# Attention product of a transformer block on one core: token blocks in twos with seven products, the second layernorm's statistics for two chunks at once, and the last weight look-ups moved beside the first part of the down projection

## The chip, the core and the metric

The kernel runs on one core of a Trainium2 chip. The core has engines with queues of their own, which work at the same time and wait for each other through semaphores: TensorE (PE in the profile; PEld are its weight loads), VectorE (DVE), ScalarE (ACT), GpSimd (POOL) and SyncE (SP). Each queue runs its instructions in the order in which they were written. DMA transfers are issued from the SP, ACT and POOL queues. TensorE writes to PSUM, which is read and written by DVE and ACT as well; the rest of the work lies in SBUF, and larger intermediate results go through DRAM.

The metric is the time of one execution on the device in microseconds, the median of several runs. The profile is one further execution, with its own time.

## The reference

All tensors are fp32, `x` is (2, 2048, 512). What is computed, cut to what matters:

```python
def attention(x, Wq, Wk, Wv, Wo):          # x: layernorm of the input
    q, k, v = x @ Wq, x @ Wk, x @ Wv
    qT, kT, vT = swapaxes(q), swapaxes(k), swapaxes(v)
    scores = einsum('bes,bfs->bef', qT, kT) / sqrt(16)
    out = einsum('bef,bfs->bes', softmax(scores), vT)
    return swapaxes(out) @ Wo

def ffn(x, lut, gate_idx, up_idx, down_idx):    # a weight is lut[idx], 16 values
    h = silu(x @ lut[gate_idx].T) * (x @ lut[up_idx].T)      # 1376 features
    return h @ lut[down_idx].T

x = x + attention(layernorm(x), Wq, Wk, Wv, Wo)
x = x + ffn(layernorm(x), lut, gate_idx, up_idx, down_idx)
```

The scores are taken between features (512 x 512 per batch), not between tokens. So attention can be folded into one 512 x 512 matrix for each batch.

## The kernel before

**Tiling.** The 4096 tokens of the two batches are 8 chunks (`NCH`) of 512 tokens, each of 4 blocks (`J`) of 128 tokens; 32 blocks (`NBLK`) in all, four chunks to a batch. `x` stays in SBUF throughout. A "512-column" operand is 128 partitions by 512 fp32.

**Stages, in order on PE.**
1. The first layernorm (class `Norm`, L185), and from its result n the Gram matrix n^T n of each batch.
2. Four 512 x 512 products per batch (class `Square`, `square()`), each by seven products of half size in place of eight (Strassen's scheme in Winograd's form), with the softmax in between. The last ones give m, one matrix per batch (`m_sb`).
3. The y stage: for each block, y = n m is added to x. `y_product` (L834) issues four matmuls of 128 x 512, with a transposed block of n as the weights; `n_turned` makes that block by a DVE transpose (`turn`, L823) of what `n_load` read back from DRAM (`nd`). 32 blocks make 128 matmuls. `added` (L843) adds y to x on DVE (L846), which also leaves the row sum `total`. From that the second layernorm's statistics are made on ACT, in `Norm.sums`: the mean (`mul`, L211), and a Square with an accumulated sum (L212). After each fourth block there is one square root (L216), then `rest` (a few small DVE operations, L231 to L248); `f_normed` writes the normed block (L278, ACT) and stores pairs of blocks to DRAM (`xnd`, L267), `f_load` reads a chunk back on the POOL queue, and `f_turned` transposes it on DVE, which gives the operand `xb` of the next stage. `f_sums` makes sums and differences of two chunks for that stage's scheme of seven products.
4. The gate/up stage: 10 slices of 128 features (`f`) by four pairs of chunks (`p`). A unit `GateUp(f, p)` is again seven products, each of several matmuls of 128 x 512, run by `Line.run` in the order a1, c1, a4 of the unit before, a2, c2, b, a3. `units` (L1413) lists them; the first eight go (0,0), (1,0), (0,1), (0,2), (0,3), (1,1), (1,2), (1,3).
5. The `rows` stage (L1349): the last 96 features.
6. The down projection, part 0 and part 1, each for eight chunks (`Down`).

**Look-ups.** The weights of stages 4 to 6 are made from indices on DVE. A `Job` (L285) reads two blocks of indices (`fetch`, L299, a DMA on the POOL queue into a single buffer), makes a 16-bit copy on ACT (`cast`, L303), and then runs 19 steps on DVE: four preparing operations (L315 to L322), eight `leaf` operations (L330) and seven `copy_predicated` picks (L342). The generator `looked_up` yields these steps one at a time; at its sixteenth step a job issues the fetch of the next one. `jobs` (L416) sets the order: gate/up pairs 0 and 1, down 0, down 2, gate/up pair 2, down 4, the other gate/up pairs, and then down 6, 8 and 10. The down jobs' weights are stored to DRAM (`wdd`) and loaded again before the down stage.

**What sets the order.** All engines' instruction order is written out at build time. In stages 2 and 3 `pump(x)` takes look-up steps worth x units of DVE time: in the y stage 1.6 for each of the first 16 blocks and 1.0 for the other 16. `side(k)` (L902) lists what else goes beside block k. In stages 4 to 6 a planner with a clock for PE and one for DVE (`clock`) decides: `between` takes one waiting operation (`todo`), and then `fill(lead)` issues look-up steps as long as the DVE clock is not further than `lead` ahead of the PE clock. `late` (L1387) puts what remains of the y stage's work (`side(32)` to `side(39)`, transposes, sums) into `todo`. Loops of the form `while …: step()` issue look-up steps at once, whatever the planner's clock says: before the down stage, all that remain.

Of the kernel before, what the change touches and what calls it, by code (L numbers as in the profile page):

```python
# [69 lines left out]
def tile_attn_ffn(  # L70
# [47 lines left out]
    wdd = dram.tile([P, NFT, E], F32, tag="wdd", name="wdd")  # L118
# [66 lines left out]
    class Norm:  # L185
        def __init__(self, c, name, back=None):
            self.name, self.back = f"{name}{c}", back
            if back:
                self.std, self.mean = back.rstd, back.nmr
            self.rstd = const.tile([P, J], F32, tag=f"rstd_{self.name}", name=f"rstd_{self.name}")  # L190
            self.nmr = const.tile([P, J], F32, tag=f"nmr_{self.name}", name=f"nmr_{self.name}")
            self.minus, self.scale = -1.0, 1.0
# [10 lines left out]
        def sums(self, j, total, block):  # L203

            if j == 0:
                self.mv = small.tile([P, J, 2], F32, tag="mv", name=f"mv_{self.name}")
                self.r0 = small.tile([P, J], F32, tag="r0", name=f"r0_{self.name}")
                self.q = small.tile([P, J], F32, tag="q", name=f"q_{self.name}")
            mean, var = self.mv[:, j, 0:1], self.mv[:, j, 1:2]
            junk = xnp.tile([P, E], BF16, tag="junk", name=f"junk_{self.name}_{j}", bufs=1)  # L210
            nc.scalar.mul(mean, total, -1.0 / E)  # L211
            nc.scalar.activation(junk, block, AF.Square, bias=mean, accum_out=var)  # L212
            self.minus, self.scale = 1.0, 1.0 / E

        def sqrt(self, a, b):
            nc.scalar.activation(self.r0[:, a:b], self.mv[:, a:b, 1], AF.Sqrt, bias=eps_sb, scale=self.scale)  # L216
# [15 lines left out]
        def rest(self, a, b, between=lambda: None):  # L232
# [5 lines left out]

            if self.scale != 1.0:
                nc.vector.tensor_scalar_mul(var, var, self.scale)  # L240
# [4 lines left out]
            stt(nmr, mean, self.minus, rstd, ALU.mult, ALU.mult)  # L245
            if self.back:
                nc.vector.reciprocal(self.std[:, a:b], rstd)
                nc.vector.tensor_scalar_mul(self.mean[:, a:b], mean, -self.minus)  # L248

        def pair(self, j, block, quarters=False):  # L250


            if j % 2 == 0:
                self.xn = xnp.tile([P, KB, 2, P], F32, tag="xn", name=f"xn_{self.name}_{j}", bufs=2)
            to = self.xn[:, :, j % 2, :]
            if quarters:
                to = to.rearrange("p i (m a) -> p m i a", a=Q)
                block = block.rearrange("p (m i a) -> p m i a", i=KB, a=Q)
            else:
                block = block.rearrange("p (i e) -> p i e", i=KB)  # L260
            self.normed(j, block, to)
            return self.xn
# [6 lines left out]
        def undone(self, j, xn, to):  # L269
# [4 lines left out]
                bias=self.mean[:, j : j + 1], scale=self.std[:, j : j + 1],  # L274
            )

        def normed(self, j, block, to):
            nc.scalar.activation(  # L278
                to, block, AF.Identity, bias=self.nmr[:, j : j + 1],
                scale=self.rstd[:, j : j + 1],  # L280
            )
# [104 lines left out]
    def down_job(i):  # L386

        f0, rows = FT[i]
# [3 lines left out]
        def dest():  # L392
            if i < K1:
# [6 lines left out]
        def after():  # L400
            nc.sync.dma_start(wdd[:rows, i : i + k, :], made[0])
# [3 lines left out]
        turn = NFT + (i - K1) // 2  # L405
        return Job(f"wd{i}", rows, E, loads, dest, after, lambda: i < K1 or turn < 4 + ended[0])
# [9 lines left out]
    jobs = [pair_job(0), pair_job(1), down_job(0), down_job(2)]  # L416
    for f in range(2, NFT - 1):
        jobs.append(pair_job(f))
        if f == 2:
            jobs.append(down_job(4))  # L420
    jobs += [pair_job(NFT - 1), *(down_job(i) for i in range(K1, NFT, 2))]
# [87 lines left out]
    ln2 = [Norm(c, "f", back=ln1[c]) for c in range(NCH)]  # L509
# [19 lines left out]
    class Operand(dict):  # L529
# [3 lines left out]
        def new(self, tag):  # L533
            self[tag] = sums.tile([P, 2, H], F32, tag="e", name=f"{tag}_{self.name}")
            return self[tag]
# [17 lines left out]
    def right(t, name, order=("T2", "T4", "T1")):  # L553
# [3 lines left out]
        def t3():  # L557
            for tag in order:
                o.new(tag)
# [157 lines left out]
    def square(a, b, dest, name, beside, rate=(0.7,) * 7):  # L717
# [5 lines left out]
        stages = [u.a1, u.c1, last.a4 if last else lambda: None, u.a2, u.b1, u.c2, u.a3]  # L723
        for i, stage in enumerate(stages):
# [3 lines left out]
            pump(rate[i])  # L728
# [77 lines left out]
    nls, nTs, ys, xfs, fls = {}, {}, {}, {}, {}  # L806
    xb, xs = {}, {}
# [17 lines left out]
    N_AT = ("a0", "a1", "a0", "a1", "a2", "a3", "a1", "a3")  # L825

    def n_load(c):
        nls[c] = reload(room(N_AT[c], f"nl_{c}"), nd[c], nc.sync)

    def n_turned(k):  # L830
        if k < NBLK:
            nTs[k] = sums.tile([P, KB, P], F32, tag="e", name=f"nT_{k}")
            turn(nTs[k], nls[k // J][:, k % J])

    def y_product(k):
        ys[k] = bank(f"y_{k}")
        m = m_sb[k // (J * CPB)]
        for i in range(KB):
            nc.tensor.matmul(  # L839
# [926 lines left out]
```

## Time and profile before

| | |
|---|---|
| median of 3 runs | 1063.83 us (1063.69 to 1063.89) |
| profiled execution | 1064.37 us, its span 1062.6 us |
| granted TensorE clock | 1.00 |
| y stage on PE | 174.7 to 286.3 us, with the last product of the squares and 256 records of y |
| gate/up stage | 286.3 to 747.6 us |
| `rows` stage | 747.6 to 789.0 us |
| down stage | 789.0 to 1058.5 us |

A span runs from the first to the last recorded instruction of the profiled execution; what lies around it belongs to the execution's time. In the tables of stages each row has a stretch of time and its length, and then the busy time of PE, of its weight loads, and of DVE, ACT and POOL, each with the number of instructions in brackets, the granted clock, the DMA share and the rate. In a row of the groups, the text has the line of the source, the engine, the operation, the output and the inputs with their shape, and the count; after the first bar the busy time and the mean duration of one instruction in ns, after the second the idle time before them on their engine and what ended it. In a timeline each row has a start, a duration, the engine and line; "x18" stands for 18 instructions of the kind run back to back. An fp32 matmul has two records on PE.

### The profile page before, as it was taken

What the parts mean: (1) busy time and instruction counts of PE and PEld (TensorE: products, weight loads), DVE (VectorE), ACT (ScalarE), POOL (GpSimd) and SP (SyncE); (2) the same over time, 40 slices, a digit from 0 to 9 for tenths busy, and PEclk for the clock granted to TensorE, in tenths of its full rate; (3) what the DMA queues carried; (4) which work ended last, traced back from release to release, by engine and by line L of the source; (5) the groups of instructions that cost most, each with busy time, mean ns of one, the idle gap of its engine ahead of it and who ended that gap; (6) DMA issues with size and microseconds to landing.
All of it is one profiled execution on the core that took longest, in us unless ns stands there. A gap on an engine that the chain in (4) does not pass through costs nothing.

```text
span 1062.6 us, 11343 instructions
## 1 busy us (share of the span) xinstructions
PE 1055.5 (99%) x3554; PEld 661.3 (62%) x3554; DVE 803.3 (76%) x1538; ACT 385.1 (36%) x725; POOL 108.6 (10%) x160
## 2 busy tenths in 40 slices
PE   8999999999999999999999999999999999999998
PEld 5668887444444444444444444444998888888887
DVE  7888788898998897887988868849756455656554
ACT  4652532455542224444443444444222222211111
POOL 0000000012120120230141023014000000000000
PEclk9999999999999999999999999999999999999999
DMA  8650314589571366696697679569747665666773
GB/s 342 224 186 21 74 25 119 137 225 250 153 217 41 133 232 197 166 201 209 198 188 215 199 170 222 190 205 195 238 149 244 204 211 187 194 195 203 226 227 117
DMA packets 129084, 194.69 MB, mean 183 GB/s; under 512 B 18992, under 2 KB 59184, under 8 KB 127872
## 3 DMA queue, kind: packets, MB, share of 16 engines
q1 hardware_dynamic: 75904, 105.81, 31.4%
q0 software_dynamic: 15776, 39.92, 17.9%
q10 hardware_dynamic: 37344, 48.24, 14.0%
q8 instruction: 28, 0.46, 0.2%
q14 instruction: 32, 0.26, 0.1%
HBM read 111.42 MB, written 82.51 MB: 183 GB/s over the span
## 4 chain that ended last, share of the span: by engine, by line
PE 97%; DVE 1%; ACT 1%; DMA 0%; issue 0%; SPq 0%; ACTq 0%
PE a_g L1065 22%; PE a_d L1065 14%; PE y L839 10%; PE c_g L1065 8%; PE c_d L1065 7%; PE gp L522 6%; PE rows L1349 4%; PE b_d L1065 4%; PE x_g L1065 4%; PE z_g L1065 4%; PE w_g L1065 3%; PE b_g L1065 2%; PE ea_t L675 1%; PE ea_p L675 1%; PE ea_m L675 1%; PE ea_s L675 1%
## 5 line engine op out<-in xcount | busy, mean ns | idle before, releaser
L839 PE MATMUL y<-m,nT 128*128 128x512 f32 x256 | 110.2, 592 | 0.0
L342 DVE COPY_PREDICATED w<-b_w,w 128x1024 f32<-128x1024 int16 (+1 forms) x77 | 98.6, 1280 | 1.4
L839 PEld LDWEIGHTS y<-m,nT 128*128 128x128 f32 x256 | 48.5, 190 | 60.5 <-issue 57.3
L1065 PE MATMUL a_g<-xT_a,s 128*128 128x512 f32 x160 | 75.5, 594 | 0.0
L1065 PE MATMUL a_g<-xb,w 128*128 128x512 f32 x160 | 75.3, 593 | 0.0
L1065 PE MATMUL c_g<-xb,w 128*128 128x512 f32 x160 | 75.2, 592 | 0.0
L1065 PE MATMUL a_d<-dT,hs_a 128*128 128x256 f32 x288 | 72.6, 379 | 0.0
L522 PE MATMUL gp<-xn_a 128*128 128x128 f32 (+3 forms) x256 | 69.9, 434 | 1.7 <-DVE xn_a L223 1.7
L330 DVE TENSOR_SCALAR w<-idx_w,lut_x,lut_sb 128x1024 int32<-128x1024 int32 (+1 forms) x88 | 67.7, 794 | 0.2
L522 PEld LDWEIGHTS gp<-xn_a 128*128 128x128 f32 x256 | 43.9, 190 | 28.4 <-issue 15.1
L172 DVE TENSOR_TENSOR r<-r,p_d 128x256 f32<-128x256 f32 x64 | 27.1, 424 | 44.4 <-ACT p_d L181 41.5
L1065 PEld LDWEIGHTS a_d<-dT,hs_a 128*128 128x128 f32 x288 | 54.5, 189 | 7.7
L1065 PE MATMUL a_g<-xT_sq,s 128*128 128x512 f32 x120 | 56.7, 595 | 0.0
L181 ACT COPY p_d<-a_d 128x256 f32<-128x256 f32 x32 | 11.9, 372 | 121.4 <-PE a_d L1065 121.4
L1065 PEld LDWEIGHTS a_g<-xT_a,s 128*128 128x128 f32 x160 | 30.1, 190 | 38.9 <-issue 36.4
L1065 PEld LDWEIGHTS a_g<-xb,w 128*128 128x128 f32 x160 | 30.3, 190 | 38.5 <-issue 35.9
L1065 PEld LDWEIGHTS c_g<-xb,w 128*128 128x128 f32 x160 | 30.4, 190 | 38.3 <-issue 37.3
L342 DVE COPY_PREDICATED wd<-b_wd,wd 128x1024 f32<-128x1024 int16 (+1 forms) x42 | 50.7, 1208 | 0.8
L172 DVE TENSOR_TENSOR r<-r,a_d 128x256 f32<-128x256 f32 x64 | 26.8, 419 | 29.5 <-PE a_d L1065 29.5
L181 ACT COPY u<-a_g 128x512 f32<-128x512 f32 x40 | 23.4, 586 | 59.9 <-PE a_g L1065 57.3
L172 DVE TENSOR_TENSOR c<-a_g,p 128x512 f32<-128x512 f32 x40 | 27.6, 691 | 20.4 <-PE a_g L1065 19.0
L1349 PEld LDWEIGHTS rows<-last,xb 128*128 128x128 f32 x256 | 41.7, 190 | 0.5 <-issue 0.5
(357 smaller groups left out, 2086.2 us busy)
## 6 DMA issues: line engine op xcount, KB each, us to landing
hd<-h SPq DMA_DIRECT2D x80, 256.0 KB, 3.3
h<-hd SPq DMA_DIRECT2D x40, 512.0 KB, 6.3
nl<-nd SPq DMA_DIRECT2D x32, 256.0 KB, 5.8
xnd<-xn_f ACTq DMA_DIRECT2D x16, 512.0 KB, 4.6
fl<-xnd POOLq DMA_DIRECT2D x32, 256.0 KB, 6.1
xn_back<-xnd SPq DMA_DIRECT2D x32, 256.0 KB, 4.0
rd<-r SPq DMA_DIRECT2D x32, 256.0 KB, 3.2
r<-rd SPq DMA_DIRECT2D x32, 256.0 KB, 4.5
```

The costliest lines, as they stand in the source:

```text
L172: nc.vector.tensor_tensor(dest, a, b, op)
L181: nc.scalar.copy(dest, a)
L330: vec.tensor_scalar(dest.bitcast(I32), idx, lut_x[:rows, k : k + 1], lut_i[:rows, at : at + 1], ALU.bitwise_and, ALU.bitwise_xor,)
L342: vec.copy_predicated(dest, masks[level - 1], t)
L522: nc.tensor.matmul(gp[b][i][:, i * P :], xn[:, i, j % 2, :], xn[:, i:, j % 2, :], start=c % CPB == 0 and j == 0, stop=c % CPB == CPB - 1 a ...
L675: nc.tensor.matmul(ps[:, m, :], self.a[a][:, k, m * P : (m + 1) * P], self.b[b][:, k, :], start=first and m == k == 0, stop=k == 1, skip_g ...
L839: nc.tensor.matmul(ys[k], nTs[k][:, i, :], m[:, i, :], start=(i == 0), stop=(i == KB - 1))
L1065: nc.tensor.matmul(ps, lhsT, rhs, start=first and i == 0, stop=i == len(pairs) - 1, skip_group_check=not first,)
L1349: nc.tensor.matmul(ps[:, jj, :], x[:, j * P : (j + 1) * P], w, start=i == 0, stop=i == len(pairs) - 1,)
```

## The change

**The y stage.** Two blocks j and j+2 of a chunk form a pair (class `Pair`). Their two rows of n times the four quarters of m are made by seven products in place of eight, with the same scheme as the squares. Each product is two matmuls of 128 x 256: 16 pairs by 14 make 224 matmuls. A pair has one PSUM tile of three banks, from a pool `yps` with two buffers. ACT copies the running sum `a` within the tile to `c11` (after a1), to `c21` (after a2) and to `c22` (after a3); DVE adds the seventh product, `p7`, to both halves of block j+2 (`seventh`); `added(1)` and `added(0)` then add the blocks j+2 and j to x and issue their statistics on ACT. Class `Chunk` transposes a chunk's blocks and makes four sums of n for it on DVE; `m_ops` has four sums of each m, those of m_0 in the last square and those of m_1 in steps 1 to 4.

**The second layernorm.** Class `Rows` has the statistics of two chunks (eight columns) in place of one chunk's four: four square roots and four `rest` in place of eight. The values that undo the norm (reciprocal and negative mean) are made at the end of the `rows` stage (`turn_back`).

**Look-ups.** `pump` is no longer called in the y stage, and the last square's rates are mostly 0. `jobs` becomes gate/up pairs 0 to 3, down 0, the remaining pairs, down 2 to 10; down 6, 8 and 10 come in the first part of the down stage, and write into `wd2` in SBUF, with no way through DRAM. There `lead` is 1.2, and 0.7 after it. Look-up steps are issued at once after unit (0,3) until down 0 is done (ahead of the release of `xnp`), before the `rows` stage until down 4 is done, and at the beginning of the down stage's second part.

**Units.** The first eight go (0,0), (1,0), (0,1), (1,1), (0,2), (0,3), (1,2), (1,3), and `late` has other contents: what remains of the norms, transposes 8 to 31, and the sums of pairs 1 to 3. `SUMS_AT`, `f_place` and the places of `n_load` use other buffers.

The diff, cut to its core:

```diff
-    wdd = dram.tile([P, NFT, E], F32, tag="wdd", name="wdd")
+    wdd = dram.tile([P, K1, E], F32, tag="wdd", name="wdd")
...
+        def sums(self, k, total, block):
+            mean = self.mean[:, k : k + 1]
+            junk = xnp.tile([P, E], BF16, tag="junk", name=f"junk_{self.name}_{k}", bufs=1)
+            nc.scalar.mul(mean, total, -1.0 / E)
+            nc.scalar.activation(
+                junk, block, AF.Square, bias=mean, accum_out=self.var[:, k : k + 1]
+            )
+
+        def sqrt(self):
+            nc.scalar.activation(self.r0, self.var, AF.Sqrt, bias=eps_sb, scale=1.0 / E)
+
+        def rest(self):
+            r0, q, stt = self.r0, self.q, nc.vector.scalar_tensor_tensor
+            nc.vector.reciprocal(r0, r0)
+            stt(q, self.var, EPS * E, r0, ALU.add, ALU.mult)
+            stt(q, q, -0.5 / E, r0, ALU.mult, ALU.mult)
+            stt(self.rstd, q, 1.5, r0, ALU.add, ALU.mult)
+            nc.vector.tensor_tensor(self.nmr, self.mean, self.rstd, ALU.mult)
+
...
+        def turn_back(self):
+            nc.vector.reciprocal(self.rstd, self.rstd)
+            nc.vector.tensor_scalar_mul(self.mean, self.mean, -1.0)
+
...
-            if i < K1:
+            if i >= K1:
+                t = wd2[0][:, i - K1 : i - K1 + k, :]
+            elif i == 0:
                 t = xnp.tile([P, 2, E], F32, tag="wds", name=f"wd_{i}", bufs=1)
             else:
...
+            if i < K1:
+                nc.sync.dma_start(wdd[:rows, i : i + k, :], made[0])
+            done.append(i)
             yield 0.1
 
         loads = [down_idx[f0 + P * q : f0 + P * q + rows, :] for q in range(k)]
-        turn = NFT + (i - K1) // 2
-        return Job(f"wd{i}", rows, E, loads, dest, after, lambda: i < K1 or turn < 4 + ended[0])
+        turn = NFT + (i - 2) // 2
+        gate = (lambda: turn < 4 + ended[0]) if 0 < i < K1 else (lambda: i == 0 or bool(wd2))
+        return Job(f"wd{i}", rows, E, loads, dest, after, gate)
+
...
-    jobs = [pair_job(0), pair_job(1), down_job(0), down_job(2)]
-    for f in range(2, NFT - 1):
-        jobs.append(pair_job(f))
-        if f == 2:
-            jobs.append(down_job(4))
-    jobs += [pair_job(NFT - 1), *(down_job(i) for i in range(K1, NFT, 2))]
+    jobs = [pair_job(f) for f in range(4)] + [down_job(0)]
+    jobs += [pair_job(f) for f in range(4, NFT)] + [down_job(i) for i in range(2, NFT, 2)]
...
-    N_AT = ("a0", "a1", "a0", "a1", "a2", "a3", "a1", "a3")
-
-    def n_load(c):
-        nls[c] = reload(room(N_AT[c], f"nl_{c}"), nd[c], nc.sync)
-
-    def n_turned(k):
-        if k < NBLK:
-            nTs[k] = sums.tile([P, KB, P], F32, tag="e", name=f"nT_{k}")
-            turn(nTs[k], nls[k // J][:, k % J])
-
-    def y_product(k):
-        ys[k] = bank(f"y_{k}")
-        m = m_sb[k // (J * CPB)]
-        for i in range(KB):
-            nc.tensor.matmul(
-                ys[k], nTs[k][:, i, :], m[:, i, :], start=(i == 0), stop=(i == KB - 1)
...
+            def s3():
+                one, two = parts
+                self.of.update({
+                    "11": one[:, 0:2], "12": one[:, 2:4], "S3": two[:, 0:2], "22": two[:, 2:4],
+                })
+                sub(two[:, 0:2], one[:, 0:2], two[:, 0:2])
+
+            of = self.of
+            return [lambda j=j: turned(j) for j in range(J)] + [
+                s3, lambda: sub(made("S2"), of["22"], of["S3"]),
+                lambda: add(made("S1"), of["S2"], of["11"]),
+                lambda: sub(made("S4"), of["12"], of["S2"]),
+            ]
+
...
+    class Pair:
+
+
+
+
+        def __init__(self, n):
+            self.c, self.s = divmod(n, 2)
+            self.k = J * self.c + self.s
+            self.n, self.m = chunks[self.c].of, m_ops[self.c // CPB]
+            t = self.t = yps.tile([P, 3, E], F32, tag="y", name=f"y_{n}", bufs=2)
+            self.c11, self.a, self.p7 = t[:, 0, H:], t[:, 1, :H], t[:, 1, H:]
+            self.c21, self.c22 = t[:, 2, :H], t[:, 2, H:]
+
+        def mm(self, to, a, b, first=False):
+            for k in range(2):
+                nc.tensor.matmul(
+                    to, self.n[a][:, k, self.s, :], self.m[b][:, k, :],
+                    start=first and k == 0, stop=k == 1, skip_group_check=not first,
+                )
+
+        def a1(self):
+            self.mm(self.a, "11", "11", True)
+            nc.scalar.copy(self.c11, self.a)
+
+        def c1(self):
+            self.mm(self.p7, "S3", "T3")
+
+        def a2(self):
+            self.mm(self.a, "S2", "T2")
+            nc.scalar.copy(self.c21, self.a)
+
+        def b(self):
+            self.mm(self.c11, "12", "21")
+
+        def a3(self):
+            self.mm(self.a, "S1", "T1")
+            nc.scalar.copy(self.c22, self.a)
+
+        def c2(self):
+            self.mm(self.c21, "22", "T4")
+
+        def a4(self):
+            self.mm(self.a, "S4", "22")
+
+        def seventh(self):
+            to = block(self.k + 2).rearrange("p (e h) -> p e h", e=2)
+            add(to, to, self.p7.unsqueeze(1).to_broadcast([P, 2, H]))
+
+        def added(self, i):
+            k, of = self.k + 2 * i, self.t[:, 2, :]
+            if not i:
+                of = self.t[:, 0:2, :].rearrange("p b e -> p (b e)")[:, H : H + E]
+            total = small.tile([P, 1], F32, tag="total", name=f"total_{k}")
+            nc.vector.scalar_tensor_tensor(
+                block(k), of, 1.0, block(k), ALU.mult, ALU.add, accum_out=total
             )
-
...
-    for k in range(NBLK):
-        if k:
-            n_turned(k + 1)
-        y_product(k)
-        if k == 0:
-            before[0].a4()
-            n_turned(1)
-            n_load(1)
+        0: turns_of(0, 2), 1: turns_of(0, 2), 2: [lambda: n_load(1), *turns_of(0, 2)],
+        3: [*turns_of(0, 1), m_ops[0].todo[0]], 4: [m_ops[0].todo[1]],
+        5: [*turns_of(0, 1), m_ops[0].todo[2]], 6: [m_ops[0].todo[3]],
+    }, (0.7, 0.7, 0, 0, 0, 0, 0), final=True)
+    pps.release()
+    yps = tc.alloc_tile_pool(name="yps", bufs=1, space=PSUM, reuse_waits="tile")
+
+    def norms(n):
+
+        i, at = divmod(n - 4, 4)
+        ops = []
+        if at == 0 and 0 <= i < NPR:
+            ops.append(ln2[i].sqrt)
+        if at == 1 and 0 <= i < NPR:
+            ops.append(ln2[i].rest)
+        i, at = divmod(n - 6, 4)
+        if 0 <= i < NPR:
+            ops += [lambda k=2 * J * i + 2 * at + q: f_normed(k) for q in range(2)]
+        c = (n - 8) // 2
+        if n % 2 == 0 and 0 <= c < NCH:
+            ops.append(lambda: f_load(c))
+        return ops
+
+    turned_at = {10: [0], 11: [1], 12: [2], 13: [3], 14: [4, 5, 6], 15: [7]}
+    summed_at = {15: 2}
+    NST = NBLK // 2
+    y = None
+    for n in range(NST):
+        work = turns_of(n // 2 + 1, 4) if n // 2 + 1 < NCH else []
+        if 1 <= n < 5:
+            work.append(m_ops[1].todo[n - 1])
+        work += [lambda k=k: f_turned(k) for k in turned_at.get(n, ())]
+        work += [lambda: next(f_pairs[0])] * summed_at.get(n, 0)
+        side = norms(n)
+        last, y = y, Pair(n)
+        y.a1()
+        if work:
+            work.pop(0)()
+        if last:
+            last.c2()
+            last.a4()
+            last.added(1)
+        if n % 2 == 0 and n // 2 + 2 < NCH:
+            n_load(n // 2 + 2)
+        y.a2()
+        if last:
+            last.added(0)
+        if work:
+            work.pop(0)()
+        if n == NST - 1:
+            y.c1()
+            y.a3()
+            y.b()
         else:
-            if k % J == 3 and k // J + 2 < NCH:
-                n_load(k // J + 2)
-            side(k)
-        pump(1.6 if k < LAG else 1.0)
...
+    next(f_pairs[0])
+    next(f_pairs[0])
+    for n, k in zip(((16,), (17,), (18,), (19,), (20, 21), (22,), (), ()), range(2 * J, 4 * J)):
+        late(normed=n, turned=[k])
+    for p in range(1, NPR):
+        late(pair=p)
+        late(pair=p)
+        late(pair=p, times=2)
+        if p == 1:
+            late(turned=[16, 17])
+            late(turned=[18, 19])
+            for k in range(20, 24):
+                late(turned=[k])
+        elif p == 2:
+            for k in (24, 26, 27, 28, 30):
+                late(turned=[k, k + 1] if k in (24, 28, 30) else [k])
 
 
...
-    units = [(0, 0), (1, 0), (0, 1), (0, 2), (0, 3), (1, 1), (1, 2), (1, 3)]
+    units = [(0, 0), (1, 0), (0, 1), (1, 1), (0, 2), (0, 3), (1, 2), (1, 3)]
...
-        if (f, p) == (1, 1):
+        if (f, p) == (0, 3):
+            while 0 not in done:
+                step()
...
+    while K1 - 2 not in done:
+        step()
...
-    while step() is not None:
-        pass
-    assert next(lookup, 0) == 0
 
...
-    leads[0] = 0.7
+    leads[0] = 1.2
...
-                nc.sync.dma_start(wd2[0][:, : NFT - K1 - 1, :], wdd[:, K1 : NFT - 1, :])
-                nc.sync.dma_start(wd2[0][:LAST, NFT - K1 - 1, :], wdd[:LAST, NFT - 1, :])
+            if (part, c, jj) == (1, 0, 0):
+                while step() is not None:
+                    pass
+                assert next(lookup, 0) == 0
+                leads[0] = 0.7
             if (part, c, jj) == (0, NCH - 1, 0):
+                while NFT - 3 not in done:
+                    step()
```

## The prediction

> **What bounds the kernel now.** I read the busy totals and the chain of waits first, then the table by stage, then the timeline around y and around the squares.
>
> ```profile
> PE 1055.5 (99%) x3554; PEld 661.3 (62%) x3554; DVE 803.3 (76%) x1538; ACT 385.1 (36%) x725; POOL 108.6 (10%) x160
> ...
> PE 97%; DVE 1%; ACT 1%; DMA 0%; issue 0%; SPq 0%; ACTq 0%
> ```
> ```profile
> 174.70:286.30 111.60, 111.60 (x265) 49.89 (x264) 100.93 (x222) 54.01 (x126) 15.30 (x27) 1.00 0.72 183
> 286.30:747.60 461.30, 461.30 (x1074) 202.99 (x1074) 384.56 (x579) 189.97 (x322) 89.18 (x121) 1.00 0.68 187
> ```
> The chain is PE from end to end, at clock 1.00. In the y stage (first row: length; then PE, PEld, DVE, ACT, POOL) PE has no gap, with DVE busy 101 of 112 us. So PE work saved is time saved, but only while nothing else makes PE wait: any wait adds in full.
>
> One place of the squares shows PE waiting for a copy that stands behind other work in ACT's queue:
>
> ```profile
> 116.96 1.67 PE L675 MATMUL ea_s<-p,S_wq 128*128 128x256 f32 x7
> ...
> 117.35 0.71 ACT L746 ACTIVATE a<-a,nb 128x512 f32<-128x512 f32 x1
> ...
> 118.05 0.56 ACT L687 COPY a<-ea_s 128x512 f32<-128x512 f32 x1
> ...
> 118.67 0.94 PEld L675 LDWEIGHTS ea_s<-T_p,S_wq 128*128 128x128 f32 x5 [0.43 <-ACT a L687]
> ```
> The copy could not start before the exponential ended, and PE began 0.06 us after the copy.
>
> **Prices.** From the y stage, the groups and the DMA list:
>
> ```profile
> 208.65 7.89 PE L839 MATMUL y<-m,nT 128*128 128x512 f32 x18
> ...
> 212.03 0.20 ACT L211 ACTIVATE mv_f<-total 128x1 f32<-128x1 f32 x1
> ...
> 212.26 0.72 ACT L212 ACTIVATE junk_f<-x,mv_f 128x512 bf16<-128x512 f32 x1
> ...
> 212.98 0.80 ACT L278 ACTIVATE xn_f<-x,nmr_f,rstd_f 128x512 f32<-128x512 f32 x1
> ...
> 214.53 0.65 DVE L846 SCALAR_TENSOR_TENSOR x<-y,x 128x512 f32<-128x512 f32 x1
> ...
> 215.12 1.53 DVE L330 TENSOR_SCALAR w<-idx_w,lut_x,lut_sb 128x1024 int32<-128x1024 int32 x2
> 215.23 0.20 ACT L211 ACTIVATE mv_f<-total 128x1 f32<-128x1 f32 x1 [1.45 <-DVE x L846]
> ```
> ```profile
> L839 PE MATMUL y<-m,nT 128*128 128x512 f32 x256 | 110.2, 592 | 0.0
> L342 DVE COPY_PREDICATED w<-b_w,w 128x1024 f32<-128x1024 int16 x70 | 91.4, 1306 | 1.3
> L172 DVE TENSOR_TENSOR c<-a_g,p 128x512 f32<-128x512 f32 x40 | 27.6, 691 | 20.4 <-PE a_g L1065 19.0
> L181 ACT COPY p_d<-a_d 128x256 f32<-128x256 f32 x32 | 11.9, 372 | 121.4 <-PE a_d L1065 121.4
> L303 ACT CAST b_w<-idx_w 128x1024 int16<-128x1024 int32 x10 | 10.4, 1041 | 2.2 <-DMA idx_w<-in_up_idx_dram 0.9 <-ACT xn_f L278 0.6 <-ACT xn_a L278 0.6
> ```
> ```profile
> idx_w<-in_up_idx_dram POOLq DMA_DIRECT2D x9, 256.0 KB, 5.0
> ```
> A matmul has two records. 512 columns: (7.89 − 0.592)/17 = 0.429 us a record, 0.858 a matmul. 256 columns, from the x7 line and the page's 379 ns for one: (1.67 − 0.379)/6 = 0.215, 0.432 a matmul. Hand-overs: a DVE add's start to ACT's mul 0.70 (214.53 to 215.23); mul and Square until ACT's next operation 0.95 (212.03 to 212.98); ACT end to PE 0.05; PE end to DVE or ACT 0.20 to 0.27, ACT end to DVE 0.03 and DVE end to PE 0.06 (starts against ends elsewhere in the same timeline). Leaf to leaf (1.53 − 0.805, one leaf's mean) 0.72, a pick 1.20 (its start to the next one's) to 1.31.
>
> **1. The products.** 128 matmuls of 512 columns become 224 of 256: 128 × 0.858 = 109.9 us become 224 × 0.432 = 96.8. Minus 13.1 us, 6.05 us of PE a step (one step is one pair of blocks, seven products of 0.864).
>
> **2. The hand-overs inside a step.** In the changed kernel's instruction order PE runs a1(n), c2(n−1), a4(n−1), a2(n), c1(n), b(n), a3(n). All of a pair lies in one PSUM tile of three banks, and an instruction waits for the last one of another engine that touched the tile. Two waits close a ring:
> - c2(n−1) waits for `seventh` on DVE, which waits for the copy to c22 on ACT, which waits for a3(n−1): 0.20 + 0.37 + 0.03 + 0.69 + 0.06 = 1.35 us. Only a1(n), 0.86, covers it: PE waits 0.49.
> - c1(n) waits for the copy to c21. On ACT that copy stands behind mul and Square of `added(1)`, which waits for a4(n−1). From a4's end: 0.25 + 0.70 + 0.95 + 0.37 + 0.05 = 2.32 us, covered by a2(n), 0.86: PE waits 1.46. Queued behind c1 are b and a3, and so the next c22 copy: the next step's wait is not shortened.
>
> The copy to c11 is covered by c2 and a4 (1.73), in even steps too, with two `normed` (0.80 each) and the `xnd` issue of some 0.5 in front of it, though only just. The `nl` loads stay 32 on SP, two chunks ahead (5.8 us to land): 0. A step takes 6.05 + 0.49 + 1.46 and some 0.1 for two restarts, whose first weight load is not hidden: 8.1 us. Neither engine is the bound (by these rows DVE has 4.6 to 5.9 us a step, ACT 4.6 to 4.9); the ring is. Between `seventh` and `added(1)` DVE also has three or four operations of 0.6 to 0.7 (the four transposes and four new sums of the next chunk over two steps): in steps 1 to 4 (sums of the second m) and 10 to 12 (a transpose) a fourth one makes `added(1)` late by 0.4, the `rest` in steps 5 and 9 by 0.65 each, step 13's by 1.25: 7 × 0.4 + 1.3 + 1.25 = 5.4 us.
>
> Sum of the stage: 0.85 at the start (the first copy waits for the last work of m_1), step 0, which has no other pair to cover its copies, 4.32 + 1.3 = 5.6; 15 × 8.1 = 121.5; 5.4; 3.1 for the last c2, a4 and adds. Together 136.4, against 109.9: plus 26.5 net, that is 39.6 of waits against 13.1 saved. Lower end: both adds' hand-overs at their smallest readings, no restarts and no late DVE work, 15 × 7.7 and 2 for those extras, 127 (+17). Upper: 0.3 us more a step, 142 (+32).
>
> The Trainium skill (Perfetto Trace Analysis, § Matmuls) says that independent matmul groups should rotate through PSUM banks so that ACT and DVE empty one while the next runs. The 0.43 us wait above is this case's own instance of what else happens. By the rule the pairs' two tiles would hide the copies, and the stage would be PE's 97 us; but four of the seven products of a pair go through one bank here, so the rule speaks against this layout. No number of the sum needs it.
>
> **3. The look-ups forced after unit (0,3).** With no look-ups in y, the loop that completes the first `down` job must issue its 15 remaining steps (8 leaves, 7 picks) at once: 8 × 0.72 + 7 × 1.25, some 14.6 us of DVE, which no unit covers in PE's order. But DVE is not what is late first: the next job's index fetch, on POOL, waits for the last leaf, the twelfth of these steps (8 × 0.72 + 4 × 1.25 = 10.8 us), and DVE first has four adds of 0.69 of unit (0,3): 13.5 us after that unit's a3. Issue 0.54, landing 5.0, the cast 1.04, and behind the cast on ACT a 512-column copy, 0.59, which PE's c2 of unit (1,2) waits for: 20.7. PE runs out of work after four products of 4 × 0.429, 6.86 us. Wait: 14. If the fetch landed early, DVE's backlog would still hold unit (1,2)'s a4 by some 11; late picks, 17.
>
> **4. The rest.** Eight `sqrt`/`rest` sets become four (0.3 and some 1 us each, off PE): 0. Transposes and sums moved from y into the first gate/up units, and the normed blocks of y's end waiting for two xn buffers until `xnd` is stored (4.6 us for 512 KB): DVE there has 385 of 461 us, 0 to 5, I take 2. The look-ups beside `down`'s first part, about 41 us of DVE (three jobs) where that engine is at 151 of 269 us over the stage: 0 to 6, I take 1; where the planner is late, the flush at that part's end pays 1.2 a pick. Their index fetches come behind the gate/up ones on POOL and are no longer followed by stores on SP and a load of `wd2`: hidden behind PE, 0. The row stage loses its look-ups, where PE is full anyway: 0.
>
> Sum: 1062.6 − 13.1 + 39.6 + 14 + 2 + 1 = 1106.1 span. The profiled run was 1064.37 with that span, the median 1063.83, 1.2 above it: **1107**.
>
> **The rivals.**
> - A, the forced look-ups are absorbed (the fetch lands in time and PE has other work): 1107 − 14 = 1093. For it: DVE idles 77 us in gate/up. Against: the queues are strict and the order is fixed. 0.13.
> - B, y costs what PE costs: 96.8 + 4 at its ends, and only the forced steps are paid: 1063.8 − 9 + 14 + 3 = 1072. For it: the copies are 0.37 and ACT is idle half the stage. Against: the order of ACT's queue. 0.04.
> - C, the other side: the copies and adds are hidden in y and the forced steps too: 1063.8 − 13.1 + 4 = 1055. What decides is the step: at 6.7 us the stage is 0.85 + 4.32 + 15 × 6.7 + 1.7 = 107.4 and 2.5 us are left for everything behind it; above that, or with a forced block over 3, the gain is gone. For it: PE alone needs 6.05. Against: point 2. 0.05.
> - D, DVE falls behind in gate/up and in `down`, and PE waits there in many places: +8 to +15, 1115 to 1122. For it: 41 us of look-ups and bunched transposes. Against: from `f` = 2 on, the planner is where it was. 0.06.
>
> **How the numbers follow.** The main case 0.72, at 1107, own range 1096 to 1118; A 0.13, B 0.04, C 0.05, D 0.06. The low end 1089 takes in A and the lower end of y with 11 of forced steps; the high end 1119 holds the upper ends of y and of the forced steps with most of D. Less than 0.2% (2.1 us) can't be told from no change here; B's and C's edges leave 0.02 for it. Faster 0.05, same 0.02, slower 0.93.
>
> **What would show it.** y: 97 us of PE in about 136, with some 1.5 us before c1 put down to ACT and 0.5 before c2 put down to DVE, step by step; if PE's idle there is under 15 us, ring and price are wrong. After unit (0,3): DVE full with L330/L342 for about 15 us and one gap of PE of 11 to 17 us, ended by ACT. Gate/up from `f` = 2 and `rows`: as before. `down`: PE idle under 6 us. A PE gap elsewhere of over 5 us would make the forecast wrong.

## The result, and the profile after

| | before | changed |
|---|---|---|
| median | 1063.86 us (1063.69 to 1063.96, 4 runs) | 1120.68 us (1119.62 to 1122.28, 4 runs) |
| ratio, with 95% interval | | 1.0536 (1.0517 to 1.0554) |
| profiled execution, span | 1064.37, 1062.6 | 1119.62, 1117.6 |
| first gate/up record, from the span's start | 286.3 | 312.9 |
| gate/up stage | 461.2 | 488.5 |
| `rows` stage | 41.6 | 41.6 |
| down stage | 269.8 | 271.1 |

A stage is counted here from its first record on PE to the first of the next one (down to its last), in us of the profiled execution; before, down runs from 789.2 to 1058.9 by this count.

The change makes the kernel 5.4% slower. The forecast was slower too, 1107 us with a range up to 1119; the time lies 1.7 us above that range. Stage by stage it was 26.5 us in y (forecast 26.5), 27.3 in gate/up (forecast 16), 0 in `rows` (forecast 0) and 1.3 in down (forecast 1).

The busy totals and the chain of the changed kernel:

```profile
PE 1058.1 (95%) x3746; PEld 695.9 (62%) x3746; DVE 833.1 (75%) x1558; ACT 397.6 (36%) x769; POOL 106.7 (10%) x160
...
PE 86%; DVE 6%; ACT 4%; DMA 2%; issue 1%; SPq 0%; ACTq 0%; POOL 0%; DVEq 0%
```

Before, 97% of the chain was PE. Now ACT, DVE and a DMA have 12% of it. The list of waits of PE (in all, times, longest) says where:

```profile
PE y L915 <- ACT y L929: 23.4, 16, 2.6
PE c_g L1216 <- ACT p L181: 11.7, 1, 11.7
PE a_g L1216 <- ACT b_g L181: 9.6, 1, 9.6
PE y L915 <- DVE x L172: 5.5, 16, 0.9
```

Two waits come in each of the 16 steps of y, and two long ones in the first gate/up units. By stage (y, then gate/up; length, then PE, its weight loads, DVE, ACT, POOL, and the clock):

```profile
176.30:312.90 136.60, 106.15 (x449) 82.16 (x450) 76.14 (x162) 62.06 (x163) 8.73 (x16) 1.00 0.46 114
312.90:801.40 488.50, 466.24 (x1073) 204.19 (x1072) 402.34 (x602) 193.24 (x327) 92.32 (x128) 0.98 0.65 182
```

In y, DVE is busy 76 of 137 us and ACT 62: no engine is full, PE waits all the same. In gate/up the clock is no longer 1.00.

**One step of y** in the changed kernel's timeline:

```profile
200.85 1.13 PE L915 MATMUL y<-T_m,nT 128*128 128x256 f32 x4 [0.31 <-DVE x L172]
201.82 1.03 PE L915 MATMUL y<-m,S_n 128*128 128x256 f32 x4
...
202.68 1.03 PE L915 MATMUL y<-T_m,S_n 128*128 128x256 f32 x4
203.10 0.69 DVE L953 SCALAR_TENSOR_TENSOR x<-y,x 128x512 f32<-128x512 f32 x1
...
203.83 0.20 ACT L263 ACTIVATE mean_f<-total 128x1 f32<-128x1 f32 x1 [2.89 <-DVE x L953]
204.07 0.72 ACT L264 ACTIVATE junk_f<-x,mean_f 128x512 bf16<-128x512 f32 x1
...
204.79 0.36 ACT L929 COPY y<-y 128x256 f32<-128x256 f32 x1
...
205.20 0.48 PE L915 MATMUL y<-m,nT 128*128 128x256 f32 x1 [1.50 <-ACT y L929]
```

Read from the top: c2 of the last pair after a short wait for DVE, then a4; a2 of the new pair; `added(1)` on DVE, the statistics on ACT, and only behind them the copy to c21, for which c1 has waited 1.50 us.

**The first long wait**, in unit (1,0), as the timeline and the DMA list (one store, issued at 327.06) show it:

```profile
336.76 1.52 ACT L283 ACTIVATE xn_f<-x,nmr_f,rstd_f 128x512 f32<-128x512 f32 x2 [5.85 <-DMA xnd<-xn_f]
...
338.31 0.52 ACTq L289 DMA_DIRECT2D xnd<-xn_f  x1
338.87 0.57 ACT L181 COPY b_g<-a_g 128x512 f32<-128x512 f32 x1 [0.59 <-ACT xn_f L283]
...
339.49 1.22 PE L1216 MATMUL a_g<-xT_a,s 128*128 128x512 f32 x1 [9.60 <-ACT b_g L181]
```
```profile
xnd<-xn_f ACTq DMA_DIRECT2D x1, 512.0 KB, 9.7
```

ACT could not write the last normed blocks before a store had freed one of the two `xn` buffers; that store took 9.7 us from issue to landing. PE's product needed a copy that stood behind those blocks in ACT's queue. The forecast had this place with 0 to 5 us.

**The second long wait**, in unit (1,2), after the forced look-ups:

```profile
411.03 0.54 POOL L319 DMA_DIRECT2D idx_w<-in_up_idx_dram  x1
414.15 1.04 ACT L323 CAST b_w<-idx_w 128x1024 int16<-128x1024 int32 x1 [14.64 <-DMA idx_w<-in_up_idx_dram]
...
415.10 0.58 ACT L181 COPY p<-c_g 128x512 f32<-128x512 f32 x1
...
415.73 1.22 PE L1216 MATMUL c_g<-xT_sq,w 128*128 128x512 f32 x1 [11.74 <-ACT p L181]
```

This is the chain of the forecast, link by link: fetch, cast, copy, c2. The first record after each long wait lasts 1.22 us where 0.59 is usual; e7 takes that up.

### The profile page after: what moved, and what is told of

The parts are those of the page before. It is cut to its first block, busy times and chain, and to the rows that moved or that the text cites. A ratio compares the mean times of both kernels' runs of the same rounds, so it can differ in the third digit from the quotient of the medians.

```text
span 1117.6 us, 11778 instructions
## 1 busy us (share of the span) xinstructions
PE 1058.1 (95%) x3746; PEld 695.9 (62%) x3746; DVE 833.1 (75%) x1558; ACT 397.6 (36%) x769; POOL 106.7 (10%) x160
## 3 DMA queue, kind: packets, MB, share of 16 engines
q0 software_dynamic: 15776, 39.92, 16.6%
## 4 chain that ended last, share of the span: by engine, by line
PE 86%; DVE 6%; ACT 4%; DMA 2%; issue 1%; SPq 0%; ACTq 0%; POOL 0%; DVEq 0%
PE a_g L1216 20%; PE a_d L1216 13%; PE c_g L1216 8%; PE c_d L1216 7%; PE gp L546 6%; PE y L915 5%; PE rows L1500 4%; PE b_d L1216 4%; PE x_g L1216 4%; PE z_g L1216 4%; PE w_g L1216 3%; PE b_g L1216 2%; DMA xnd<-xn_f 1%; PE ea_t L701 1%; ACT junk_f L264 1%; PE ea_m L701 1%
## 5 line engine op out<-in xcount | busy, mean ns | idle before, releaser
L1216 PE MATMUL a_g<-xT_a,s 128*128 128x512 f32 x240 | 115.1, 603 | 9.6 <-ACT b_g L181 9.6
L1216 PEld LDWEIGHTS a_g<-xT_a,s 128*128 128x128 f32 x240 | 45.6, 192 | 68.9 <-issue 54.6
L915 PE MATMUL y<-m,nT 128*128 128x256 f32 x192 | 48.7, 389 | 24.5 <-ACT y L929 23.4
L915 PEld LDWEIGHTS y<-m,nT 128*128 128x128 f32 x192 | 35.0, 190 | 35.7 <-ACT y L929 29.8
L181 ACT COPY p_d<-a_d 128x256 f32<-128x256 f32 x32 | 11.9, 371 | 121.7 <-PE a_d L1216 121.7
L172 DVE TENSOR_TENSOR x<-x,y 128x512 f32<-128x512 f32 x16 | 11.0, 688 | 57.6 <-ACT y L936 54.2
L181 ACT COPY u<-a_g 128x512 f32<-128x512 f32 x40 | 23.4, 585 | 56.9 <-PE a_g L1216 55.0
```

The costliest lines, as they stand in the source:

```text
L172: nc.vector.tensor_tensor(dest, a, b, op)
L181: nc.scalar.copy(dest, a)
L915: nc.tensor.matmul(to, self.n[a][:, k, self.s, :], self.m[b][:, k, :], start=first and k == 0, stop=k == 1, skip_group_check=not first,)
L1216: nc.tensor.matmul(ps, lhsT, rhs, start=first and i == 0, stop=i == len(pairs) - 1, skip_group_check=not first,)
```

## The experiments

The edits are against the changed kernel unless said otherwise. Medians of 4 runs where no number is given, beside 1063.6 to 1063.9 of the kernel before.

**e1: the copy ahead of the statistics.**

```diff
             last.a4()
-            last.added(1)
...
         y.a2()
         if last:
+            last.added(1)
             last.added(0)
```

> Only ACT's order in the y stage is changed: the copy to c21 is issued ahead of the statistics of the block that `added(1)` finished. Theory (ring): c1 then waits only for the copy, 0.20 + 0.37 + 0.05 = 0.62 us a step in place of the 23.4 us that the profile of the changed kernel puts down to that copy in 16 waits: 15 x 0.62 = 9.3, so some 14 us less, 1106 to 1108 us, and the wait of c2 for DVE (5.5 us in all) stays. Rival (DVE's adds or the shared PSUM tile hold c1, and the copy's place is chance): within 3 us of the changed kernel, 1118 to 1123.

Measured: 1104.07 us (ratio 1.0371, 1.0354 to 1.0389), 16.6 less than the changed kernel; the first gate/up record comes at 297.0 in place of 312.9. PE's waits in y:

```profile
PE y L915 <- ACT y L929: 8.0, 16, 0.5
PE y L915 <- DVE x L172: 5.5, 16, 0.8
```

The wait before c1 falls from 23.4 to 8.0 us, 0.5 a step, and the one before c2 stays. It was the place of the copy in ACT's queue; the rival is out.

**e2: the hand-overs covered.** c21 and c22 in a tile of their own, a4 of the last pair after a2, and one normed block behind each of the first two copies.

```diff
-            t = self.t = yps.tile([P, 3, E], F32, tag="y", name=f"y_{n}", bufs=2)
+            t = self.t = yps.tile([P, 2, E], F32, tag="y", name=f"y_{n}", bufs=2)
+            u = self.u = yps.tile([P, E], F32, tag="u", name=f"yu_{n}", bufs=2)
...
         y.a1()
+        for op in normed[:1]:
+            op()
...
             last.c2()
-            last.a4()
-            last.added(1)
...
         y.a2()
+        for op in normed[1:]:
+            op()
         if last:
+            last.a4()
+            last.added(1)
             last.added(0)
```

> The y stage with the hand-overs covered: c21 and c22 in a PSUM tile of their own, PE's order a1, c2 of the pair before, a2, a4 of the pair before, c1, b, a3, and each copy of ACT ahead of the statistics and of one of the two normed blocks. Theory (all waits of the stage come from the ring, and PE's 96.8 us are the floor): the stage falls from 136.6 us to 101 to 106, the time to 1085 to 1090. Rival (ACT or DVE is itself too full at 6.05 us a step, so that the waits come back elsewhere): the stage at 115 to 130, 1100 to 1115.

Measured: 1086.53 us (1.021, 1.0194 to 1.0225). The y stage by itself:

```profile
176.00:280.80 104.80, 99.27 (x449) 83.58 (x449) 75.81 (x162) 62.10 (x163) 10.66 (x20) 1.00 0.62 151
```

The same DVE and ACT work as before the edit (76 and 62 us) now fits into 104.8 us, and the first gate/up record comes at 280.8, 5.5 us earlier than in the kernel before. So the saving in products is real; the changed kernel spent it, and 26.5 us more, on hand-overs. Not all of the theory's "97" is reached: PE still waits 2.4, 1.5 and 1.1 us for ACT in a few steps.

**e5: e2 with one tile.** The same order, `yps.tile([P, 3, E], …)` as in the changed kernel.

> The kernel of e2 with all of a pair in one PSUM tile again, so that only the order of PE and ACT differs from the changed kernel. Theory (c2 touches the tile that `seventh` reads, so with one tile it waits 0.3 us a step for DVE, and c22's copy in front of it is what e2's second tile leaves): e2 plus 15 x 0.3 to 0.5 = 5 to 8 us, 1091 to 1095. Rival (the order alone does it, the tile's split nothing): 1085 to 1088, as e2.

Measured: 1095.09 us (1.0289, 1.0273 to 1.0305), 8.6 more than e2.

```profile
PE y L915 <- DVE x L172: 7.8, 16, 0.9
```

c2 waits for `seventh` again, in all 16 steps; in e2, with two tiles, that row is gone. By the medians this is a little more than the 5 to 8 expected. In the profiles it is 115.3 us from the last record of the squares to the first of gate/up, against e2's 105.1; 7.8 of the 115.3 are this wait, and some 1.7 are a clock that this execution halved at y's end (last section). So the split is worth some 8 us; the order alone doesn't do it.

**e3: down 0 ahead of gate/up pair 3.**

```diff
-    jobs = [pair_job(f) for f in range(4)] + [down_job(0)]
-    jobs += [pair_job(f) for f in range(4, NFT)] + [down_job(i) for i in range(2, NFT, 2)]
+    jobs = [pair_job(f) for f in range(3)] + [down_job(0)]
+    jobs += [pair_job(f) for f in range(3, NFT)] + [down_job(i) for i in range(2, NFT, 2)]
```

> One change in the list of look-ups: down 0 is looked up ahead of gate/up pair 3, so that it is done by unit (0,3) and nothing is left to force there. Theory (the forced steps alone make PE's 11.7 us wait in unit (1,2), and the slow clock after it costs 2.0 more): 13 to 14 us less, 1106 to 1108. Rival (DVE is behind anyway, and pair 3's steps make the same wait in another place): within 4 us of the changed kernel.

Measured: 1112.1 us (1.0451, 1.0435 to 1.0466), 8.6 less, not 13 to 14. The 11.7 us wait is gone, but the timeline has a new one in unit (2,1), where the sums of pair 3 are first needed:

```profile
439.93 1.13 PE L1216 MATMUL z_g<-T_c_in,lc 128*128 128x512 f32 x2 [3.15 <-DVE lc L172]
```

Another 1.6 us lie in y, where this profile has a slower clock after a 2.57 us wait (below). Of the theory and its rival each is true in part: the forced steps made the large wait, and DVE is also some 3 us late with pair 3.

**e4: the last norms spread out.**

```diff
-    for n, k in zip(((16,), (17,), (18,), (19,), (20, 21), (22,), (), ()), range(2 * J, 4 * J)):
+    for n, k in zip(((16,), (17,), (), (18,), (), (19,), (), (20,)), range(2 * J, 4 * J)):
...
-        late(pair=p)
+        late(pair=p, normed=[21] if p == 1 else [])
...
-            late(turned=[16, 17])
+            late(turned=[16, 17], normed=[22])
```

> The normed blocks of the last two pairs of chunks, which the changed kernel issues in consecutive places of the first gate/up units, go into every second place. Theory (ACT is held by the two buffers xn until the store of xnd has landed, 5.9 us, with PE's copy b_g behind it): the 9.6 us wait of PE and the 3.0 us of slow clock after it go, 1107 to 1110. Rival (ACT simply has too much to do there, normed, statistics and the load of its table): less than 4 us gained, 1116 to 1121.

Measured: 1111.88 us (1.045, 1.0435 to 1.0466), 8.8 less; the gate/up stage falls from 488.5 to 480.0. The 9.6 us wait is gone, one of 2.7 us behind ACT is left in its place, and `rows` has 1.5 us more (one wait of 1.3 us for DVE). More than the rival's 4, less than the 11 to 14 expected.

**e6 and e9: the read-back later.** e6 issues `f_load` of chunks 4 to 7 as items of their own behind the first sums of pair 1:

```diff
-        if n % 2 == 0 and 0 <= c < NCH:
+        if n % 2 == 0 and 0 <= c < 4:
             ops.append(lambda: f_load(c))
...
         if p == 1:
+            for c in range(4, NCH):
+                f_later(c)
```

> The changed kernel with the read-back (`f_load`) of chunks 4 to 7 issued only after all stores of the normed blocks; stores and normed blocks stay bunched. Theory A (the stores are slow, 9.7 us to land against 4.7, because the read-back's 1 MB at a time shares the DMA engines): the longest store lands in under 7 us, PE's wait for b_g falls from 9.6 to under 6. Theory B (two buffers for eight bunched blocks are enough for the wait, whatever the DMA engines carry): it stays at 8 to 10 us, and the time within 3 of the changed kernel.

e9 issues those of 7, 5 and 6 in this order after the last norms (`c < 5`, and at n = 22 the three loads):

> e6 left the read-backs where they were in time, so this one puts them behind the stores by POOL's own order: the read-back of chunk 7, which must wait for the last store, stands ahead of those of chunks 5 and 6. Theory A (a store is slow because a read-back shares the DMA engines with it): the store that took 9.7 us, issued some 9 us after y's last products, lands in 3 to 5 us; ACT's wait of 5.9 us goes, and PE's wait for b_g falls from 9.6 to 4 to 5. Theory B (the bunched stores slow each other): the store still takes 8 us or more, and PE waits 9 to 10. Later DVE will wait for the chunks that now come late, so the whole time says nothing.

Measured: 1121.2 us (1.0538, 1.0523 to 1.0552) and 1122.27 (one run), PE's wait 9.7 us in both. Neither tells the theories apart. The built program's POOL queue still has chunk 5's read-back in its old place, and its timeline shows it at 326.7 and 326.9 us, 12.3 and 12.4 us after the first gate/up record, as in the changed kernel (325.2 and 312.9, 12.3). In e6 chunk 5's read-back had nothing but earlier read-backs ahead of it on POOL, and went when its data were there. In e9 it stands behind chunk 7's in the source, and the built queue has it ahead all the same: where an operation stands in the source did not set where the build put it.

**e11: no read-back of chunk 5.**

```diff
     def f_load(c):
-        fls[c] = reload(room(f"x{c}", f"fl_{c}"), xnd[c], nc.gpsimd)
+        t = room(f"x{c}", f"fl_{c}")
+        if c != 5:
+            fls[c] = reload(t, xnd[c], nc.gpsimd)
+            return
+        nc.gpsimd.memset(t, 0.0)
...
```

> e6 and e9 did not move the read-back of chunk 5 in time. This one leaves it out: the second layernorm's blocks of chunk 5 are zeros in the gate/up stage (set by GpSimd, off the path). Theory A (the store that takes 9.7 us shares the DMA engines with this read-back): it lands in 3 to 5 us, ACT's wait of 5.9 us for a buffer goes, and PE's wait for b_g falls from 9.6 to 3 to 5, 5 to 8 us less in all with what the clock then keeps. Theory B (the bunched stores slow each other): the store still takes 8 us or more and PE waits 9 to 10.

Measured: 1115.3 us (one run). The same store (here issued at 328.52) in the DMA list, and PE's wait:

```profile
xnd<-xn_f ACTq DMA_DIRECT2D x1, 512.0 KB, 3.2
```
```profile
PE a_g L1224 <- ACT b_g L181: 4.3, 1, 4.3
```

9.7 us become 3.2, ACT's wait for the buffer is gone, and PE's wait falls from 9.6 to 4.3: theory A. What is left of it is ACT's own work ahead of that copy. The gate/up stage falls from 488.5 to 482.8, 5.8 us; the whole time falls by less, because this execution halved the clock once in y (1.7 us; last section).

**e7: the second wait filled with PE work.**

```diff
             mm(self.a, self.pairs("S2", "T2"), False)
+            if (self.f, self.p) == (1, 2):
+                for _ in range(6):
+                    for lhsT, rhs in self.pairs("S2", "T2"):
+                        nc.tensor.matmul(self.a, lhsT, rhs, start=False, ...)
```

> The changed kernel with six extra repeats of a2's product in unit (1,2), 6 x 1.716 = 10.3 us of PE work laid into the 11.7 us wait; gate and up of that slice and chunk pair get wrong sums by it. Theory (PE's clock is halved because PE idles): the first records after the wait stand 0.43 us apart in place of 0.85, the remaining wait is 1.4 to 2 us, and unit (2,0) begins 2 us earlier than in the changed kernel, counted from y's end. Rival (the slow records come from the operands or from DMA traffic beside them): they stay at 0.85.

Measured: 1117.47 us (one run). The first 4 us after that wait, in the changed kernel and then in e7:

```profile
415.60:419.60 4.00, 3.87 (x5) 1.80 (x6) 3.33 (x8) 1.06 (x3) 1.63 (x4) 0.51 0.73 268
```
```profile
415.60:419.60 4.00, 3.82 (x9) 1.82 (x10) 3.97 (x10) 1.19 (x4) 1.65 (x4) 1.00 0.74 271
```

Five records at clock 0.51 against nine at 1.00, beside the same DMA traffic (268 and 271 GB/s). The slow records come from PE's idling. In the changed kernel they cost 2.0 us after the 11.7 us wait and 2.5 after the 9.6 (sum of the spacings over 0.429). With the repeats PE still waits 1.6 us, and the gate/up stage takes 486.9 us, 1.7 less than in the changed kernel where 2 were expected.

**e8, e10, e12: together.** e8 is e2, e3 and e4 in one.

> e2, e3 and e4 together. Theory (three separate causes that add): 1120.7 - 34.1 - 8.6 - 8.8 = 1069, some 1066 to 1073; the rest over the kernel before is the 3.1 us wait that e3 showed, the 2.7 of e4, 1.4 in `rows` and 1.3 in the down stage, less some 5.5 gained in y. Rival (they overlap, or the faster y pushes more stores into the same place): over 1075.

Measured: 1067.62 us (5 runs; 1.0037, 1.0025 to 1.005). The three causes add. What is left of PE's waits in gate/up, from its list:

```profile
PE z_g L1222 <- DVE lc L172: 3.1, 1, 3.1
...
PE a_g L1222 <- ACT h L1384: 1.5, 1, 1.5
```

e10 has the norms in every second place, up to the sums of pair 1, and

```diff
+        if n in (0, 6, 7, 8, 9, 13):
+            pump(0.7)
```

at the end of the steps of y.

> e8 with the last norms in every second place through to the sums of pair 1, and one look-up step at the end of six of the steps of y, where DVE has room. Theory (e8's 3.1 us wait is DVE being 3 us late with gate/up pair 3 at unit (2,1), its 1.5 us wait a store): both go, 1062 to 1065. Rival (the steps make y's ring late instead, or stores still block ACT): 1066 to 1070.

Measured: 1061.51 us (9 runs; 0.9976, 0.9967 to 0.9986). Both waits are gone; gate/up takes 462.4 us, 1.2 more than before.

> e10 with a lead of 2.0 in place of 1.2 for the look-ups beside the first part of down. Theory (the last 0.6 us wait in down is the last look-up job ending late): that wait goes, 0.5 to 1 us less than e10, 1060 to 1061. Rival (DVE, at some 85% there, then makes PE wait for its sums): 1062 to 1065.

Measured, with `leads[0] = 2.0`: 1060.40 us (9 runs; 0.997, 0.996 to 0.998), the lowest median here, 3.2 us under the kernel before; the single runs of e10 (1060.4 to 1062.5) and e12 (1059.5 to 1061.5) overlap. The 0.6 us wait is gone from PE's list, and down falls from 271.1 to 270.2. Its totals:

```profile
PE 1046.8 (99%) x3746; PEld 696.3 (66%) x3746; DVE 828.5 (78%) x1558; ACT 398.2 (38%) x769; POOL 106.8 (10%) x160
```

PE's busy time is 8.7 us under the kernel before (1055.5), and PE is full again.

## Why the prediction was wrong

**Point 1, the products: right.** A product of two matmuls shows as 0.86 us between waits, and e2 reaches 104.8 us for the stage.

**Point 2, the ring: right in mechanism, and right in size by luck.** The stage was to cost 26.5 us more and cost 26.5 us more. The two waits are where they were forecast, but both were counted too high. c1's wait was 23.4 us in 16 steps, where 1.46 for each of 15 and 5.4 for late DVE work had been counted; 1.16 to 1.83 in most steps and 2.57 once leave about 1 us for late DVE work. c2's was 0.30 to 0.36 in 15 steps and 0.85 in the last, not 0.49. What made up for this is the restart after a wait, for which 0.1 a step had been counted, 1.5 in all: PE is busy for 106.15 us in the stage, while 448 records at 0.215 take 96.3. So nearly 10 us lie in records that take longer, most of them the first two after a wait. e1 takes away most of c1's wait, and e2's second tile takes away c2's.

**Point 3, the forced look-ups: right in sum, by two errors.** The forecast was a wait of 14. The wait was 11.7: the chain is as told, but from the first index fetch's issue to the cast it took 3.65 us (410.50 to 414.15), not 5.5. The missing 2.0 came back as slow clock, which the forecast did not have at all. e3 removes the wait and shows what the forecast did not see, that pair 3 is then 3.1 us late.

**Point 4, the step that failed:** "the normed blocks of y's end waiting for two xn buffers until `xnd` is stored (4.6 us for 512 KB) ... 0 to 5, I take 2". The place is right, the size is not: 9.6 us of wait and 2.5 of slow clock after it, a wait of 0.9 us for DVE's moved sums in the unit before it, and some 0.16 of restart for each wait, 13.4 in all. Against 2, these 11.4 us are nearly the whole difference between the forecast span (1106.1) and the measured one (1117.6). The forecast had named a gap of PE of over 5 us in another place as the sign of being wrong; this is one. Two things were missed.
- The median of 4.6 us hid two kinds of store. The trace of the kernel before already had them: the store issued at 281.3 landed in 3.2 us, the one issued at 223.9, behind a read-back, in 10.0:

```profile
xnd<-xn_f ACTq DMA_DIRECT2D x1, 512.0 KB, 10.0
```

  In that kernel's y stage a store had some 7 us until the next, and ACT waited 0.4 us in all for one. With the stores bunched, one of the slow kind meets the last free buffer; e11 shows it by taking the read-back away.
- What stood behind the waiting instruction was not named: PE's copy b_g. The term was priced by what DVE had to spare in gate/up (385 of 461 us busy), and not as a wait of PE.

**The clock.** A long wait of PE costs more than its length. The Trainium skill (TensorE: Matmul & The Clock Gate, § Part 1: The HAM clock gate) says that the array falls to half rate after an idle window of some 3.4 us. The runs agree with it in part: after each of the 17 waits of 4.3 to 11.9 us in these profiles, records stand 0.85 us apart, and the granted clock is a half, for 3.0 to 6.1 us. But in six of the 17 the clock was a half from 2.0 to 2.4 us after the wait began, sooner than 3.4 us. Short waits don't fit a plain threshold either; see the last section.

**The rest.** The median lies 3.1 us above the profiled span, where 1.2 was taken over from before. The four runs fall into two pairs, 1119.6 to 1119.8 and 1121.6 to 1122.3. A clock that halves in y in some executions would make such a step: the profiles of e6 (1121.61) and e9 (1122.27), which have the changed kernel's y stage, show it there, with y at 138.3 and 138.2 us in place of 136.6. But no profile of the slower pair itself was taken. Down (1.3 against 1) and `rows` (0) were as forecast. Of the rivals, C, the one on the other side, needed steps under 6.7 us: they took 8.2 to 8.7, once 9.5 (from one c1 to the next). D placed its waits of DVE in many places of gate/up; there is none from unit (2,0) on. Three slips of the forecast's sums moved nothing that mattered: two records of 0.215 make 0.430 and not 0.432 (0.4 us over the stage), 8 × 0.72 + 7 × 1.25 is 14.5 and not 14.6, and 0.3 us more in 15 steps puts y's upper end at 140.9 and not 142.

## What to carry to other kernels

A product saved on the bounding engine is worth its time only if each hand-over around it is covered by other products: list what stands ahead of every copy in its engine's queue, and put the copies that release the bounding engine ahead of work that nobody waits for. Where a step makes transfers come in a bunch, price them by their slowest instances beside the same traffic, not by their median, and name the instruction behind the one that will wait. For a long wait of PE, add the slow restart.

## What the runs showed of the hardware

After waits of 4.3 us (e11) and of 7.9 us or more, PE's granted clock was a half for 3.0 to 6.1 us in every profile, 1.6 to 3.1 us lost. When it fell differs: 5.2 us after the wait began in e11's wait of 4.3 us (so 0.95 us after its end), 4.3 and 5.3 us after it in the changed kernel's two, and from 2.0 to 2.4 us after it in six waits of other runs. One of these is e9's, in which PE was idle from 331.5 to 341.2; the clock is the third number from the end:

```profile
331.60:333.60 2.00, 0.00 (x0) 0.00 (x0) 2.00 (x4) 0.94 (x2) 0.00 (x0) 1.00 0.94 218
333.70:341.20 7.50, 0.00 (x0) 0.00 (x0) 4.83 (x6) 2.12 (x4) 0.55 (x1) 0.50 0.78 239
```

After waits of 2.7 and 3.1 us (e4, e3) it stayed at 1.00. But the same wait of 2.57 us in step 14 of y, itself a stage in which PE waited in each step, was followed by full clock in the changed kernel, e4 and e7, and by half clock in e3, e6, e9 and e11, whose y stages are 1.6 to 1.7 us longer. In e5 the clock fell to a half near y's end, after waits of 0.8, 1.5 and 0.9 us within 9 us. The 4 us around the 2.57 us wait's end, in the changed kernel, then in e3:

```profile
298.40:302.40 4.00, 3.72 (x16) 2.96 (x16) 0.65 (x2) 2.00 (x7) 1.34 (x3) 1.00 0.80 191
```
```profile
298.20:302.20 4.00, 3.91 (x10) 3.17 (x11) 0.00 (x0) 0.98 (x4) 1.36 (x3) 0.58 0.82 186
```

Sixteen records against ten. So one and the same wait can cost its length, or 1.7 us more. It seems that several short waits close together can do what a long one does, but what decides it is open.

A 512 KB store of normed blocks took 3.2 us at best, and mostly 5 to 10 when a read-back of a chunk (1 MB in four transfers, on another queue) had been issued in the 3 us before it, in the kernel before as in the changed one. For one of them e11 shows the read-back to be the cause (9.7 to 3.2); for the others it is only what stands beside them. And it isn't the only thing that goes with a slow store: those issued at 243.6 and 259.9 in the changed kernel took 5.3 us with no read-back in the 4 us before them.
